# A four-layer graph network on one core: node work in two halves, two tables of range sums, clears at other places, empty tiles left out

## The chip, the cores and the metric

The kernel runs on one core of a Trainium2 chip. The metric is device time in microseconds (us) of one execution; a number of runs is given as the median of its executions. Engines are named as in the profile: PE (TensorE matmul), PEld (its weight loads), DVE (VectorE), ACT (ScalarE), POOL (GpSimd), SP (SyncE); "SPq" and "ACTq" are the instructions that start a transfer.

## What is computed

There are 12,500 nodes of 32 features and 400,000 edges, sorted by their destination dst. Each of four layers normalizes the nodes, forms a message for each edge from the source node's row, and adds the messages up by destination:

```python
h = relu(layernorm(x)); x = x + (1 + eps) * h + segment_sum(relu(h[src] + edge_attr_32), dst)      # layer 0
h = relu(layernorm(x)); x = x + L1(h, src, dst, edge_attr_3, edge_attr_10, edge_weight)            # layer 1
h = relu(layernorm(x)); x = x + L2(h, src, dst)                                                    # layer 2
h = relu(layernorm(x)); x = x + L3(h, src, dst, edge_attr_4, edge_attr_8)                          # layer 3
```

Layer 1 is an equivariant tensor product (tanh gates, weights of a small network on edge_attr_10, sums by dst). Layer 2 is a graph convolution with normalized degrees: `norm * (segment_sum((norm * h)[dst], src) + norm * h)`, `norm = rsqrt(1 + deg)`, where deg counts how often a node is a source; its sums go by source. Layer 3 is a product like layer 1's with a hidden layer of 256 and a factor 1 / sqrt(E / N).

## The kernel before

**Nodes.** x and h stay in SBUF as 125 partitions x 100 nodes x 32 features (`self.x`, `self.h`; `NP` = 125, `J` = 100). `norm_relu` (L415) is eight DVE operations and one ACT square over all of them, each of the large ones on 125 x 3200 elements; it ends with a store of h to a table `feats[l]` in HBM (L444), from which the edges gather rows. With `by_part` the features are stored in another order, by two copies (L440, L441).

**Edges.** They are cut into 196 windows of 16 tiles of 128 edges; four tiles are a group. There are 3125 tiles that hold edges; the last window has 5 of them. For each tile POOL issues one indirect transfer that gathers 128 rows (L617 in layer 0, L907 in the fused loop of layers 1 and 2, L1380 in layer 3); in layer 0, in most windows, the last two tiles are instead picked from a table in SBUF with 14 nodes to a line (`table`, L583 to L586, and `from_table`). In the fused loop POOL also issues one scatter with add per tile (L1108), to tables of layer 2 by source.

**Sums.** As the edges are sorted, a window's destinations lie in a range of at most 128 nodes. PE adds the messages of a window up with a one-hot matrix (`collect`, L468), and `put_late` (L495, transfer L498, on ACT's queue) writes 128 rows of the result to a table in HBM, `tabs[l][no % TABS[l]]`, at the window's first node. Neighbouring windows overlap, so they go to different tables: four in layers 0, 2 and 3, two in layer 1 (there `put`, L493, on SP). Tables are cleared first (`clear`, L393: five transfers of 125 x 640 zeros and a tail, L396 and L397, on ACT's queue). After a loop `gather_sum` (L448) loads the layer's tables, in turn on SP and ACT (L452), and adds them (L455); `end0`, `end1`, `end2` and `end3` add the sum to x (L1353 in layer 3), and `out` is stored at L1354.

**Order.** `setup` loads x; `norm_relu(0)` follows; `windows` (L256) loads dst (L265), works out each window's first node and a flag that says whether the fast form of the loops may run (widths and distances of windows, L284 to L304), and the program branches on it. In the branch `layer0` first takes four steps of the generator `rest`, the clears of layer 0's tables, and builds `table`; then it runs `edges` (L655). That loop loads two windows ahead, gathers four groups ahead, and takes one step of `rest` at each second group: the other ten tables' clears, then weights, places, unit vectors and parts of the embeddings for the later layers. The instructions of an engine are put in order by a scheduler that goes by their dependencies; for POOL in layer 3 the written order is kept. Then follow `norm_relu(1)`, `degrees`, the store of `mid` (x and degrees by node, L806), the fused loop `edges12`, `end1`, `norm_relu(2)` (which starts while layer 2's scatters still run), `end2`, `norm_relu(3)`, the loop `edges3`, `end3`. In `edges3` a window passes through `scalars`, `product` (L1425 to L1435), `outputs` (L1441 to L1449), `thirds` (L480 to L484), `collect` and `add`, in four steps each.

Of the kernel before, what the change touches and what calls it, by code (L numbers as in the profile page):

```python
# [16 lines left out]
P = 128  # L17
# [11 lines left out]
TABS = {0: 4, 1: 2, 2: 4, 3: 4}  # L29
ROUND = 12582912.0  # L30
PIECES = 5
# [30 lines left out]
class GNN:  # L62
# [47 lines left out]

    def rows_for(self, t, n, c, t0):

        k = max(0, min(n, self.filled(c) - t0))
        if k < n:
            self.nc.vector.memset(t[:, k:n, :], 0.0)
        return range(k)

    def nodes(self, ap):
        return ap.rearrange("(p j) d -> p (j d)", p=NP)


    def setup(self):
# [3 lines left out]
        nc.sync.dma_start(self.x.rearrange("p j d -> p (j d)"), self.nodes(self.a["x"]))  # L126
# [31 lines left out]

        self.none = keep.tile([P, D + 1], F32, name="none")
# [80 lines left out]
    def rest(self, pool):  # L240

        nc, J = self.nc, self.J
        zero = pool.tile([P, J * D // PIECES], F32, name="zero")
        nc.vector.memset(zero, 0.0)
        for l in range(4):
            for t in self.tabs[l][: TABS[l]] if self.fast else self.tabs[l]:
                self.clear(t, zero)
                yield
        yield from self.weights(pool)
        if self.fast:  # L250
            yield from self.places_by_edge(pool)
            yield from self.unit_vectors(pool)
            yield from self.parts_of(pool, self.a["ea10_c"], self.emb10)
            yield from self.parts_of(pool, self.a["ea8_c"], self.emb8)

    def windows(self):  # L256
# [4 lines left out]
        with ExitStack() as ctx:  # L261
# [3 lines left out]
            nc.scalar.dma_start(dst.rearrange("p w t -> p (w t)"), self.a["dst"])  # L265
            first = pool.tile([P, NW], F32, name="first")
# [29 lines left out]
            nc.vector.tensor_reduce(top[:, 0:1], loc, AX.XY, ALU.max)  # L296
# [9 lines left out]
            nc.vector.tensor_scalar(flag, worst, float(P), None, op0=ALU.is_lt)  # L306
        return nc.values_load(flag[0:1, 0:1], min_val=0, max_val=1)
# [85 lines left out]
    def clear(self, t, zero):  # L393
        n = self.J * D // PIECES
        for k in range(PIECES):
            self.nc.scalar.dma_start(self.nodes(t[: self.N])[:, n * k : n * k + n], zero[:NP])  # L396
        self.nc.scalar.dma_start(t[self.N :], zero[:, :D])  # L397

    def rsqrt(self, pool, v, shape):

        nc = self.nc
        n = v.shape[0]
        r = pool.tile(shape, F32, name="rs_r")
        t = pool.tile(shape, F32, name="rs_t")
        r, t = r[:n], t[:n]
        nc.scalar.activation(t, v, AF.Sqrt)
        nc.vector.reciprocal(r, t)
        nc.vector.tensor_mul(t, r, r)
        nc.vector.tensor_mul(t, t, v)
        nc.vector.tensor_scalar(t, t, -0.5, 1.5, op0=ALU.mult, op1=ALU.add)  # L410
        nc.vector.tensor_mul(r, r, t)
        return r


    def norm_relu(self, l, scale=None, by_part=False, store=True):  # L415


        nc, J = self.nc, self.J
        with self.tc.tile_pool(name=f"norm{l}", bufs=1) as pool:
            def wide(s):  # L420
                return s[:, :, None].to_broadcast([NP, J, D])

            m = pool.tile([NP, J], F32, name="m")
            nc.vector.tensor_reduce(m, self.x, AX.X, ALU.add)
            nc.vector.tensor_scalar_mul(m, m, 1.0 / D)
            nc.vector.tensor_tensor(self.h, self.x, wide(m), op=ALU.subtract)
            sq = pool.tile([NP, J, D], F32, name="sq")
            nc.scalar.activation(sq, self.h, AF.Square)
            v = pool.tile([NP, J], F32, name="v")
            nc.vector.tensor_reduce(v, sq, AX.X, ALU.add)  # L430
            nc.vector.tensor_scalar(v, v, 1.0 / D, 1e-5, op0=ALU.mult, op1=ALU.add)
            r = self.rsqrt(pool, v, [NP, J])
            if scale is not None:
                nc.vector.tensor_mul(r, r, scale)
            nc.vector.tensor_mul(self.h, self.h, wide(r))
            nc.vector.tensor_scalar_max(self.h, self.h, 0.0)
            h = self.h
            if by_part:
                h = sq
                nc.vector.tensor_copy(h[:, :, 0:8], self.h[:, :, 0:8])  # L440
                nc.vector.tensor_copy(h[:, :, 8:32].rearrange("p j (i u) -> p j u i", i=3),  # L441
                                      self.h[:, :, 8:32].rearrange("p j (u i) -> p j u i", i=3))
            if store:
                nc.sync.dma_start(self.nodes(self.feats[l][: self.N]), h.rearrange("p j d -> p (j d)"))  # L444

    def gather_sum(self, l, pool):

        nc = self.nc  # L448
        parts = []
        for k, t in enumerate(self.tabs[l][: TABS[l] if self.fast else NTAB]):  # L450
            s = pool.tile([NP, self.J, D], F32, name=f"part{k}")
            (nc.sync, nc.scalar)[k % 2].dma_start(s.rearrange("p j d -> p (j d)"), self.nodes(t[: self.N]))  # L452
            parts.append(s)
        for part in parts[1:]:
            nc.vector.tensor_add(parts[0], parts[0], part)  # L455
        return parts[0]


    def collect(self, l, pool, psum, c, feat, t0):
# [7 lines left out]
        for k in range(G):  # L467
            nc.tensor.matmul(c["sum"], lhsT=oh[:, k, :], rhs=feat[:, k, :], start=t0 + k == 0, stop=t0 + k == self.CT - 1)  # L468
        if t0 + G == self.CT:
# [4 lines left out]
    def thirds(self, pool, c, step):  # L474

        nc = self.nc
        if step == 0:
            c["f3"] = pool.tile([P, self.CT, 3, D], BF16, name="f3")
# [177 lines left out]
    def edges(self, load, gather, front, main, tail, begin=None, windowed=None, beside=None):  # L656
# [4 lines left out]
        with self.tc.For_i(0, self.T // IT, 1) as it:  # L661
            i = it * IT
            n = CPI * CG
# [3 lines left out]
            def fetch(g):  # L667
                c, k = divmod(g, CG)
                if k == 0:
                    for c1 in range(len(chunks), min(c + 1 + (LEAD if self.fast else 0), CPI)):  # L670
# [3 lines left out]
                        chunks[c1]["no"] = c1  # L674
                        if windowed:
# [32 lines left out]
    def layer0(self):  # L708
# [5 lines left out]
        with ExitStack() as ctx:  # L714
            rest = None
            if self.fast:
                self.resident(ctx)
                rest = self.rest(ctx.enter_context(tc.tile_pool(name="rest", bufs=1)))
                for _ in range(TABS[0]):
                    next(rest)  # L720
# [39 lines left out]
            def tail(c, t0, m):  # L760
# [21 lines left out]
                for k in range(G):  # L782
                    nc.tensor.matmul(c["deg"][:NP, :J], lhsT=ohi[:, k, :], rhs=olo[:, k, :],
                                     start=t0 + k == 0, stop=t0 + k == self.CT - 1)
                if t0 + G == self.CT:
# [6 lines left out]
        with tc.tile_pool(name="end0", bufs=1) as pool:  # L792
            agg = self.gather_sum(0, pool)
            nc.vector.tensor_add(self.x, self.x, agg)
            nc.vector.scalar_tensor_tensor(self.x, self.h, self.eps1, self.x, op0=ALU.mult, op1=ALU.add)

    def layers12(self):

        nc, J = self.nc, self.J
        self.norm_relu(1, by_part=True)  # L800
# [7 lines left out]
        self.end1()  # L808
        self.norm_relu(2, scale=self.deg, store=False)
        self.end2()  # L810

    def layer1(self):
        self.norm_relu(1)
        self.any1()
        self.end1()
# [9 lines left out]
    def end2(self):  # L825
        nc, J = self.nc, self.J
        with self.tc.tile_pool(name="end2", bufs=1) as pool:
            agg = self.gather_sum(2, pool)
            nc.vector.tensor_add(agg, agg, self.h)
            nc.vector.tensor_mul(agg, agg, self.deg[:, :, None].to_broadcast([NP, J, D]))  # L830
            nc.vector.tensor_add(self.x, self.x, agg)

    def end1(self):
        with self.tc.tile_pool(name="end1", bufs=1) as pool:
            self.nc.vector.tensor_add(self.x, self.x, self.gather_sum(1, pool))
# [476 lines left out]
    def layer2(self):  # L1312
        nc, tc = self.nc, self.tc
        self.degrees()
        self.norm_relu(2, scale=self.deg)
# [27 lines left out]
        self.end2()  # L1343

    def layer3(self):
        nc = self.nc
        with ExitStack() as ctx:
            if self.fast:
                self.resident(ctx)
            self.norm_relu(3, by_part=self.fast)  # L1350
            (self.edges3 if self.fast else self.any3)()
        with self.tc.tile_pool(name="end3", bufs=1) as pool:
            nc.vector.tensor_add(self.x, self.x, self.gather_sum(3, pool))  # L1353
        nc.sync.dma_start(self.nodes(self.out), self.x.rearrange("p j d -> p (j d)"))  # L1354

    def edges3(self):

        nc, tc, CT = self.nc, self.tc, self.CT
        with ExitStack() as ctx:
# [36 lines left out]
            def scalars(c, g, i):  # L1396

                if (g, i) == (0, 0):
                    c["q"] = wp.tile([P, CT, 16], F32, name="q", bufs=3)
                    c["dd"] = wp.tile([P, CT, 3, 8], F32, name="dd", bufs=3)  # L1400
                    c["vv"] = wp.tile([P, CT, 3, 8], F32, name="vv", bufs=3)
                gs = slice(G * g, G * g + G)
# [10 lines left out]
            def dots(c):  # L1413
                nc.vector.tensor_reduce(c["q"][:, :, 8:16], c["dd"].rearrange("p g k u -> p g u k"), AX.X, ALU.add)

            def product(c, g):

                if g == 0:
# [18 lines left out]
            def outputs(c):  # L1437
                sh = c["sh"]
                f = c["f"] = wp.tile([P, CT, D], F32, name="f")
                fv = f[:, :, 8:32]  # L1440
                nc.vector.tensor_reduce(f[:, :, 0:8], c["pa"], AX.X, ALU.add)  # L1441
                nc.vector.tensor_reduce(fv.rearrange("p g (w i) -> p g i w", i=3),  # L1442
                                        c["pv"].rearrange("p g i (w u) -> p (g i) w u", u=8), AX.X, ALU.add)
                rs = wp.tile([P, CT, 8], F32, name="rs", bufs=1)
                nc.vector.tensor_reduce(rs, c["ps"], AX.X, ALU.add)  # L1445
                t1 = wp.tile([P, CT, 8, 3], F32, name="t1", bufs=1)
                nc.vector.tensor_mul(t1, rs[:, :, :, None].to_broadcast([P, CT, 8, 3]),
                                     sh[:, :, None, 1:4].to_broadcast([P, CT, 8, 3]))
# [9 lines left out]
            def collect(c):  # L1458
                c["sum"] = ps.tile([P, B], F32, name="ps_sum")
                for k in range(CT):  # L1460
                    nc.tensor.matmul(c["sum"][: 3 * D, 0:P], lhsT=c["f3"][:, k].rearrange("p i f -> p (i f)"), rhs=c["oh"][:, k, :],  # L1461
                                     start=k == 0, stop=k == CT - 1)
# [22 lines left out]
            for c in range(NW + 1):  # L1485
# [3 lines left out]
                for s in range(4):  # L1489
# [5 lines left out]
                    if now:  # L1495
                        product(now, s)
                        places(now, 4 * s, 4 * s + 4)
# [173 lines left out]
```

## Time and profile before

| what | us |
|---|---|
| median of 4 runs | 18773.51 (18759.29 to 18782.71) |
| the profiled execution | 18764.26 |
| its span in the trace | 18762.5 |
| POOL busy in the span | 14661.1 (78%) |
| PE, DVE, ACT busy | 13498.4, 13656.4, 7248.7 |
| first gather of layer 0 / of the fused loop / of layer 3 | 74.33 / 3744.34 / 13924.30 |
| last put of layer 3, end of the span | 18680.32, 18762.5 |

The span is the time from the first to the last instruction of one profiled execution; the execution's own time is 1.8 us longer. Busy times of engines overlap. In lines of the timeline the columns are start (us), duration (us), engine, line of the kernel, operation, output<-inputs, count, and in brackets the idle time of the engine before it with what ended it ("issue": nothing that the profile shows). In lines of groups they are line, engine, operation, output<-inputs, count, then busy us and mean ns of one, then idle us before them with the main releaser.

### The profile page before, as it was taken

To read this page: it belongs to the slowest core of one execution; us is meant where nothing else is said; L and a number is where in the kernel's file an instruction comes from. 1 tells how busy PE (TensorE), PEld (TensorE's weight loads), DVE (VectorE), ACT (ScalarE), POOL (GpSimd) and SP (SyncE) were. 2 spreads that over 40 slices of the span, in tenths; PEclk is the share of its full clock that TensorE was granted. 3 is DMA by queue.
4 is the path that set the end of the run, shared out by engine and by line. 5 is a ranking of instruction groups with operands and counts; after the bars stand their busy time and mean duration, and the time that the engine had idled before them with its cause. 6 is when DMAs were issued, how large, how long until landed. Compare 5 with 4: busy or idle time off the path is not lost. (4 is left out here: it accounts for less than half of the span.)

```text
span 18762.5 us, 211174 instructions
## 1 busy us (share of the span) xinstructions
PE 13498.4 (72%) x64508; PEld 7139.8 (38%) x64508; DVE 13656.4 (73%) x26105; ACT 7248.7 (39%) x15398; POOL 14661.1 (78%) x14476
## 2 busy tenths in 40 slices
PE   5888888676666666666666666666638888888886
PEld 4555555422112121211111112111116666666665
DVE  6887766687777777777777777777747777777776
ACT  2334333233333333333333333333315555555554
POOL 5777777578888888888888888888868888888885
PEclk8888888787777777777777777777758888888888
DMA  4246422244444444444444444444431111111111
GB/s 123 64 121 194 141 38 38 48 106 92 94 92 94 91 91 92 92 94 92 94 91 91 92 91 93 93 95 91 88 63 27 26 27 26 27 26 27 26 27 33
DMA packets 1506892, 1429.22 MB, mean 76 GB/s; under 512 B 1053126, under 2 KB 1267796, under 8 KB 1452156
## 3 DMA queue, kind: packets, MB, share of 16 engines
q1 hardware_dynamic: 697752, 1170.64, 19.9%
q0 software_dynamic: 737712, 199.28, 13.6%
q10 hardware_dynamic: 70272, 45.63, 0.8%
q8 instruction: 512, 8.39, 0.2%
q14 instruction: 644, 5.28, 0.1%
HBM read 1177.50 MB, written 236.40 MB: 75 GB/s over the span
## 5 line engine op out<-in xcount | busy, mean ns | idle before, releaser
L1108 POOL DMA_INDIRECT acc<-summed,rows x3125 | 4995.5, 1599 | 993.7 <-issue 733.0
L1425 PE MATMUL ps_w<-w2b,hid 128*128 128x256 f32 x12544 | 3446.7, 433 | 833.5 <-DVE pv L1433 832.8
L907 POOL DMA_INDIRECT hs<-feat,src x3125 | 3135.6, 1003 | 1080.7 <-issue 930.6
L1380 POOL DMA_INDIRECT hs<-feat,src_all x3125 | 3053.5, 977 | 888.3 <-issue 784.4
L617 POOL DMA_INDIRECT hs<-feat,src_all x2741 | 2672.4, 975 | 940.7 <-issue 613.0
L948 PE MATMUL ps_y<-Q,w2t 64*128 64x512 f32 x4704 | 2097.6, 887 | 1806.5 <-DVE z L951 1796.9
L1425 PEld LDWEIGHTS ps_w<-w2b,hid 128*128 128x128 f32 x12544 | 2737.3, 221 | 1430.5 <-issue 872.9
L951 DVE TENSOR_TENSOR z<-ps_y,hid 128x1024 f32<-128x1024 f32 x2352 | 2852.7, 1213 | 328.1 <-PE ps_y L948 324.4
L605 PE MATMUL lined<-table,which 128*128 128x448 bf16 x8064 | 2041.1, 399 | 42.8 <-DVE picked L610 27.4
L958 PE MATMUL ps_o<-z,sums 128*32 128x512 f32 x9408 | 1955.5, 735 | 3.7 <-DVE r L963 3.2
L948 PEld LDWEIGHTS ps_y<-Q,w2t 64*128 64x128 f32 x4704 | 639.4, 261 | 2973.9 <-DVE z L951 2183.2
L922 DVE STREAM_TRANSPOSE X<-hs 128x512 f32<-128x512 f32 x392 | 270.0, 690 | 1986.8 <-DMA hs<-feat,src 1986.8
L480 ACT CAST f<-f 128x512 bf16<-128x512 f32 x784 | 479.9, 612 | 2908.1 <-DVE f L976 2671.0
L1393 ACT ACTIVATE hid<-ps_h 128x1024 f32<-128x1024 f32 x784 | 798.9, 1019 | 1670.7 <-PE ps_h L1391 1656.2
L932 ACT COPY X<-ps_m 32x512 f32<-32x512 f32 x784 | 451.5, 576 | 2553.3 <-PE ps_m L929 2522.4
L929 PE MATMUL ps_m<-has,win 128*32 128x512 f32 x1568 | 726.5, 1029 | 912.8 <-DVE has L916 772.1
L948 PE MATMUL ps_y<-X,w2t 64*128 64x512 f32 x4704 | 1260.0, 636 | 151.3 <-DVE z L951 150.2
L605 PEld LDWEIGHTS <-which 128*128 128x128 bf16 x8064 | 864.0, 117 | 703.6 <-issue 236.4
L1455 ACT ACTIVATE oh<-iota,local 128x128 bf16<-128x128 f32 x3136 | 1056.4, 391 | 49.0 <-DMA local<-local 25.9
L468 PEld LDWEIGHTS ps_win<-m,oh 128*128 128x128 f32 x6272 | 993.8, 234 | 182.3 <-issue 113.3
L983 ACT ACTIVATE oh<-iota,local 128x128 bf16<-128x128 f32 x3136 | 1014.9, 390 | 71.8 <-DMA local<-local 71.8
L468 PE MATMUL ps_win<-m,oh 128*128 128x32 f32 x6272 | 981.4, 306 | 61.9 <-DVE oh L465 33.7
(230 smaller groups left out, 21832.9 us busy)
## 6 DMA issues: line engine op xcount, KB each, us to landing
has<-loc_t SPq DMA_DIRECT2D x392, 1024.0 KB
srow<-in_src_t SPq DMA_DIRECT2D x392, 512.0 KB
N<-n_t SPq DMA_DIRECT2D x3136, 32.0 KB
hs<-feat,src_all POOLq DMA_INDIRECT x5866
emb<-pp SPq DMA_DIRECT2D x252, 280.0 KB
emb<-emb SPq DMA_DIRECT2D x196, 360.0 KB
emb<-pp SPq DMA_DIRECT2D x252, 224.0 KB
emb<-emb SPq DMA_DIRECT2D x196, 288.0 KB
```

What stands on the lines that cost most here:

```text
L468: nc.tensor.matmul(c["sum"], lhsT=oh[:, k, :], rhs=feat[:, k, :], start=t0 + k == 0, stop=t0 + k == self.CT - 1)
L605: nc.tensor.matmul(t, lhsT=c["which"][:, b, k * P : k * P + P], rhs=self.table3[:, b, i], start=(b, i) == (0, 0), stop=(b, i) == (BLOCKS - ...
L617: self.nc.gpsimd.indirect_dma_start(out=t[:, k, :], out_offset=None, in_=self.feats[l][:], in_offset=bass.IndirectOffsetOnAxis(ap=idx[:, t ...
L907: nc.gpsimd.indirect_dma_start(out=c["hs"][:, k, :], out_offset=None, in_=self.feats[1][:], in_offset=bass.IndirectOffsetOnAxis(ap=c["src" ...
L948: nc.tensor.matmul(y[:, q, :], lhsT=self.w2t[64 * q : 64 * q + 64, h, j, :], rhs=c["Q" if j < 3 else "X"][64 * q : 64 * q + 64, h, :], sta ...
L951: nc.vector.tensor_mul(z, y, c["hid"][:, 2 * h : 2 * h + 2, :])
L958: nc.tensor.matmul(c["o", j // 3][32 * q : 32 * q + 32, :], lhsT=self.sums[:, j, :], rhs=c["z", j, q % 2][:, q // 2, :], start=j % 3 == 0, ...
L983: nc.scalar.activation(c["oh"][:, k, :], self.iota, AF.Square, bias=c["local"][:, k : k + 1], scale=-1.0)
L1108: nc.gpsimd.indirect_dma_start(out=self.tabs[2][k % NTAB][:], out_offset=bass.IndirectOffsetOnAxis(ap=c["rows"][:, G * g + k : G * g + k + ...
L1380: nc.gpsimd.indirect_dma_start(out=c["hs"][:, k, :], out_offset=None, in_=self.feats[3][:], in_offset=bass.IndirectOffsetOnAxis(ap=c["src" ...
L1425: nc.tensor.matmul(w[:, k, :], lhsT=c["hid"][:, m, 4 * g + k].rearrange("p q s -> p (q s)"), rhs=self.w2b[:, m, :], start=m == 0, stop=m == 1)
L1455: nc.scalar.activation(c["oh"][:, k, :], self.iota, AF.Square, bias=c["local"][:, k : k + 1], scale=-1.0)
```

## The change

- `TABS` is {0: 2, 1: 2, 2: 4, 3: 2}: two tables in layers 0 and 3, 10 cleared in all in place of 14.
- x's load, the norm, the loads and sums of the tables, the stores of h and of the output go by two halves of 50 nodes to a partition (`halves`). `norm_relu` takes over the sum of the tables (`parts_in`, all loads on SP) and the addition to x; relu and scale are one operation, and with `by_part` four that also do the reordering.
- `windows` issues dst's load and then calls the first norm; one full reduce (L296) is replaced by one of a 128 x 196 array.
- Layer 0's two tables are cleared on ACT's queue before the flag is read; the other eight on SP's, as the last steps of `rest`, one transfer in two steps.
- `x += eps1 * h` of layer 0 stands before its loop in place of behind it; layer 2's own term is added by `own`, behind `norm_relu(2)`.
- In the last window of layers 0 and 3 groups without edges are left out (2 of 4).

The core of the diff:

```diff
-TABS = {0: 4, 1: 2, 2: 4, 3: 4}
+TABS = {0: 2, 1: 2, 2: 4, 3: 2}
+    def groups(self, c):
+
+        return max(1, -(-self.filled(c) // G))
+    def halves(self):
+        return slice(0, self.J // 2), slice(self.J // 2, self.J)
...
-        nc.sync.dma_start(self.x.rearrange("p j d -> p (j d)"), self.nodes(self.a["x"]))
+        for js in self.halves():
+            nc.sync.dma_start(self.x[:, js].rearrange("p j d -> p (j d)"), self.nodes(self.a["x"], js))
...
-        for l in range(4):
-            for t in self.tabs[l][: TABS[l]] if self.fast else self.tabs[l]:
-                self.clear(t, zero)
-                yield
         yield from self.weights(pool)
...
+        for l in range(4):
+            for t in self.tabs[l][2 if l == 0 else 0 : TABS[l] if self.fast else NTAB]:
+                for _ in self.clear(t, self.nc.sync):
+                    yield
+                    yield
...
             nc.scalar.dma_start(dst.rearrange("p w t -> p (w t)"), self.a["dst"])
+            meanwhile()
...
-            nc.vector.tensor_reduce(top[:, 0:1], loc, AX.XY, ALU.max)
+            nc.vector.tensor_reduce(top[:, 0:1], high, AX.X, ALU.max)
...
+        for t in self.tabs[0][:2]:
+            for _ in self.clear(t, nc.scalar):
+                pass
         return nc.values_load(flag[0:1, 0:1], min_val=0, max_val=1)
...
+    def norm_relu(self, l, add=None, scale=None, by_part=False, store=True):
...
+            parts = [self.parts_in(pool, add, u) if add is not None else () for u in range(2)]
+            for u, js in enumerate(self.halves()):
...
+                x, h = self.x[:, js], self.h[:, js]
+                for k, part in enumerate(parts[u][1:]):
+                    nc.vector.tensor_add(parts[u][0], parts[u][0], part)
+                if add == 2:
+                    nc.vector.tensor_mul(parts[u][0], parts[u][0], wide(self.deg[:, js]))
+                if add is not None:
+                    nc.vector.tensor_add(x, x, parts[u][0])
...
+                if by_part:
+                    turned = h[:, :, 8:32].rearrange("p j (u i) -> p j i u", i=3)
+                    for i in range(4):
+                        nc.vector.scalar_tensor_tensor(
+                            sq[:, :, 8 * i : 8 * i + 8], turned[:, :, i - 1] if i else h[:, :, 0:8], 0.0,
+                            r[:, :, None].to_broadcast([NP, n, 8]), op0=ALU.max, op1=ALU.mult)
+                    h = sq
+                else:
+                    nc.vector.scalar_tensor_tensor(h, h, 0.0, wide(r), op0=ALU.max, op1=ALU.mult)
+                if store:
+                    nc.sync.dma_start(self.nodes(self.feats[l][: self.N], js), h.rearrange("p j d -> p (j d)"))
...
+    def parts_in(self, pool, l, u):
...
+            self.nc.sync.dma_start(s.rearrange("p j d -> p (j d)"), self.nodes(t[: self.N], js))
...
-                for _ in range(TABS[0]):
-                    next(rest)
+            nc.vector.scalar_tensor_tensor(self.x, self.h, self.eps1, self.x, op0=ALU.mult, op1=ALU.add)
...
-        self.end1()
-        self.norm_relu(2, scale=self.deg, store=False)
-        self.end2()
+        self.norm_relu(2, add=1, scale=self.deg, store=False)
+        self.own()
...
-            agg = self.gather_sum(2, pool)
-            nc.vector.tensor_add(agg, agg, self.h)
-            nc.vector.tensor_mul(agg, agg, self.deg[:, :, None].to_broadcast([NP, J, D]))
-            nc.vector.tensor_add(self.x, self.x, agg)
+        nc.vector.tensor_mul(self.h, self.h, self.deg[:, :, None].to_broadcast([NP, self.J, D]))
+        nc.vector.tensor_add(self.x, self.x, self.h)
...
-            nc.vector.tensor_add(self.x, self.x, self.gather_sum(3, pool))
-        nc.sync.dma_start(self.nodes(self.out), self.x.rearrange("p j d -> p (j d)"))
+            parts = [self.parts_in(pool, 3, u) for u in range(2)]
+            for u, js in enumerate(self.halves()):
+                for part in parts[u]:
+                    nc.vector.tensor_add(self.x[:, js], self.x[:, js], part)
+                nc.sync.dma_start(self.nodes(self.out, js), self.x[:, js].rearrange("p j d -> p (j d)"))
...
             def product(c, g):
 
+                if g >= self.groups(c):
+                    return
...
-                for k in range(CT):
+                n = G * self.groups(c)
+                for k in range(n):
...
-        g.norm_relu(0)
-        ok = g.windows()
+        ok = g.windows(lambda: g.norm_relu(0))
```

## The prediction

> **What bounds the kernel now.** I read the costliest groups first. The four gather and scatter groups of POOL lead, and nearly all the idle time ahead of them is "issue", time in which POOL waited for nothing:
>
> ```profile
> POOL 5777777578888888888888888888868888888885
> L1108 POOL DMA_INDIRECT acc<-summed,rows x3125 | 4995.5, 1599 | 993.7 <-issue 733.0
> L907 POOL DMA_INDIRECT hs<-feat,src x3125 | 3135.6, 1003 | 1080.7 <-issue 930.6
> L1380 POOL DMA_INDIRECT hs<-feat,src_all x3125 | 3053.5, 977 | 888.3 <-issue 784.4
> L617 POOL DMA_INDIRECT hs<-feat,src_all x2741 | 2672.4, 975 | 940.7 <-issue 613.0
> ```
>
> The first line is POOL's busy tenths in 40 slices, the others give count, busy time, mean ns and idle time. In the timeline POOL's next instruction follows its last after 0.30 us. So inside the three edge loops POOL is full, and an edit there saves nothing unless it takes instructions from POOL. The change takes none of its 12,116 transfers away; in the order of the changed program POOL's sequence is the same, six small dropped calculations at the end apart. What can be won lies where POOL stands still: at the start, between the loops, after the last. The timeline shows these places, columns start, us, engine, line:
>
> ```profile
> 74.33 1.10 POOL L617 DMA_INDIRECT hs<-feat,src_all  x1 [72.49 <-DMA acc<-zero]
> ...
> 117.13 1.50 ACT L583 CAST table<-tv 128x448 bf16<-128x448 f32 x3 [85.58 <-DMA acc<-zero]
> ...
> 136.80 0.94 POOL L617 DMA_INDIRECT hs<-feat,src_all  x1 [32.51 <-DVE m L756]
> ...
> 3691.01 7.02 DVE L455 TENSOR_TENSOR part<-part,part 125x3200 f32<-125x3200 f32 x2 [16.80 <-DMA part<-acc]
> ...
> 3744.34 0.94 POOL L907 DMA_INDIRECT hs<-feat,src  x1 [129.45 <-ACT rs_t L406]
> ...
> 13766.97 5.34 POOL L1108 DMA_INDIRECT acc<-summed,rows  x1 [0.30 <-issue]
> ...
> 13867.64 7.02 DVE L455 TENSOR_TENSOR part<-part,part 125x3200 f32<-125x3200 f32 x2 [8.46 <-DMA part<-acc]
> ...
> 13924.30 1.01 POOL L1380 DMA_INDIRECT hs<-feat,src_all  x1 [103.89 <-DMA feat<-sq]
> ...
> 18735.80 7.02 DVE L455 TENSOR_TENSOR part<-part,part 125x3200 f32<-125x3200 f32 x2 [19.68 <-DMA part<-acc]
> ```
>
> POOL gathers from 74.33, stalls from 104.3 (its 24th gather issues at 103.35) to 136.8 because ACT's casts come late, stands from 3614.9 to 3744.3 and from 13820.4 to 13924.3, and the end follows the last sum (put at 18680.32) by 82 us. The time in these places is transfers of node arrays (125 partitions, 1.6 MB), so I looked at their rate in the table of stretches (last columns: DMA share, GB/s):
>
> ```profile
> 66.00:75.00 9.00, 0.00 (x0) 0.00 (x0) 1.55 (x12) 0.00 (x0) 0.67 (x1) 1.00 0.87 287
> 18683.00:18700.00 17.00, 0.00 (x0) 0.00 (x0) 0.00 (x0) 0.00 (x0) 0.00 (x0) 0.50 0.30 122
> ```
>
> The edge indices (128 partitions) moved at 287 GB/s; table loads with nothing beside them at 122 GB/s on 0.30 of the DMA engines, though SP and ACT both issued. A single store (out, 18746.4 to 18762.5, and feat, 3729.98 to 3743.6) needed 13.6 to 16 us. So a table costs 13.1 us, half a table 6.6, on one queue or two. The Trainium skill ("DMA: Bandwidth & Descriptors", section "Bandwidth") gives 341 GB/s at 1 MB; by that the two tables dropped at the end would be worth 9 us, not 26. Its measurement is with 128 partitions, the row with 125 decides.
>
> **Part A, the start.** Now ACT sends 24 clears of four tables from 66.33, and its casts for the table of lines wait until 117.13; the gathers hang on these from the 25th on. As 24 are done by then, POOL's effective start is 136.80 − 24 × 1.25 = 106.8. In the changed program dst is loaded ahead of the first norm, only two tables are cleared, ahead of the flag, and no clear stands ahead of the casts. x's second half lands at about 16.9 as x does now; with the first half's work done meanwhile, the norm's DVE work (16.88 to 38.91 now, less 1.83 for the fused relu) ends near 33. The flag's chain (45.42 to 64.65, 19.2 us, less 3.1: a reduce of 3.41 becomes one of 196 columns) then ends near 49. Flag to first gather takes 9.7 now: 59; plus 4 for clears that share the engines with the feat store: 63. Casts need 19.7 us from ACT free to gather (117.13 to 136.80), so they end near 75, ahead of the 24th gather (63 + 30 = 93): no stall. Gain 106.8 − 63 = 44, less 5 for table arithmetic on DVE beside gathers: **−39** (−48 without these 5 and the 4; −27 if POOL stalls 12 us more for the casts).
>
> **Part B, first loop to second.** Now: last gather done at 3614.9, last sum put at 3631.59, first part load issued 2.0 later, 6.4 MB in until 3691.0, 39 us of DVE work, store 13.6, gather at 3744.3: 129.4 us after the last gather. Changed, counted from the last gather: put at 11 (six us earlier, as two empty groups are not worked through), loads at 15, two tables as four half loads, first halves in at 30, second at 43. The merged order has half 0's sum and mean first, then waits for half 1's add, so little of half 0 runs ahead. From 43: about twelve half operations of 1.75 (half of 3.49, estimate), twice 2.2 of small ones, the copies for the order of parts now within the multiply; the two chains interleave. Half 0 stored from 55, half 1 from 63, landed 70, gather at 72.5. The product h·eps1 (3.49) goes ahead of the first loop, where DVE idles. **−57** (−45 if half 1's chain is not interleaved with half 0's square on ACT, −68 if half 0 runs ahead). POOL's one wait in the ramp behind it, 21.8 us for L1104, is due to a has load that SP issues at 3763.7, behind the mid store; in the new order it stands ahead of the feat store: **−5** (0 to −10).
>
> **Part C, second to third.** All four tables stay, now in eight half loads on SP, behind table 0's wait (issued 13831.46 now; ACT started its two 10 us earlier). Behind that wait on SP stand only the feat store and the third loop's loads, which come later anyway. In at 13831.5 + 6.4 MB / 122 GB/s = 13884, 17 us later than now; behind it half 1's share alone: nine half operations and small ones, 18, store 6.8 + 2: gather at 13911 against 13924.3, −13. Against it, own() puts two full DVE operations with two SBUF inputs in POOL's drain. Beside such operations a scatter took 5.34 (and 4.64, 4.56, 3.86) in place of 1.54: 2 × 3.4 = +7. **−6** (−16 to +8, if table 0's halves wait longer or half 1 is not helped).
>
> **Part D, the end.** Last put about 10 earlier: two of four product groups gone, and the last window's reductions (2.27 + 3.34 + 1.21 + 0.56 + 0.56 us) halved. Then loads 2.7 after the put as now, 3.2 MB in 26.4 and landing: 18701; two half adds 3.5, half a store 6.8 with half 0's in front of it done by then: about 18710 against 18762.5. **−52** (−40 to −60, as table 0 may start before the last put).
>
> **Costed at nothing.** Eight late clears, 40 transfers of 0.32 MB on SP: in the new order they stand between the edge loads of windows 9 to 14, not at the end of the loop. They take 12.8 MB / 121 GB/s = 106 us; SP runs five windows ahead (5 × 17.5 = 87), so at worst POOL stalls 19 us once. Two tables in place of four mean that a put waits for the one two windows before: 35 us, with a landing of 2.65 (put 18680.32, load 18682.97). Groups left out elsewhere lie under POOL.
>
> **Sum** −39 − 57 − 5 − 6 − 52 = **−159** (ends −104 and −202). The profiled run took 18764.3 (span 18762.5), 9 below the median of the four, 18773.5; so 18605 for a run like the profiled one, and **18614** for the median.
>
> The skill speaks against the halves ("DMA: Bandwidth & Descriptors", section "Rules for kernel authors"): transfers to halves serialise on the same engines, so don't split. The trace agrees on the engines (0.30 and 122 GB/s for two queues), but splits by partitions are meant; here the second half's transfer hides the first half's arithmetic. If splitting brought nothing, the sum would be about −115.
>
> **Rivals.**
> (1) The change does only part of what it says: halves interleave on DVE so that none runs ahead, and the "late" clears, hoisted, stall the first loop. Halves are worth 5 (A), 15 (B), 15 (C), 10 (D) by the working above; with the stall of 19: −159 + 45 + 19 = −95, **18679**. For it: half 0 waits for half 1's add in the order of part B, and SP waits for lanes in the first loop even now. Against: the last store is half as long in any order.
> (2) Slower: POOL's rows lengthen. The same gather costs 975, 977 and 1003 ns in three loops, so what stands beside it counts. Place: all 12,116 transfers; 28 ns each, the spread of these rows, is +339, so +180 net, **18954**. It decides from 159 / 12,116 = 13 ns, and is slower beyond the bound from 16. Against it: POOL's order and DVE's work inside the loops are unchanged.
> (3) The start's gain is given back, because the first loop is held by preparation on DVE or SP (77 gathers in 100 us from 1200 to 2200, 80 from 2300 to 3500, where 0.95 + 0.30 us apiece fills POOL): −120, **18654**, inside the range.
>
> **Chances.** The forecast (−125 to −200) 0.70; smaller gain, (1) and (3), 0.21; still larger 0.02; nothing left 0.03; rival (2) 0.04. Under about 0.2% (37 us) this kernel can't be told from no change: faster 0.93, same 0.03, slower 0.04. Range 18570 to 18690: the sum's ends, −202 and −104, and from there to rival (1).
>
> **What would show it.** Right: first gather near 63 and no second start; two part loads per half after 3570; about 72 us without POOL between the first loops, some 97 between the next two (after scatters stretched twice more); the last put to the end 40 us. Wrong: a POOL gap between windows 9 and 20 behind clears (1); the means of L617, L907, L1108, L1380 up by 10 ns (2); POOL's gather count per 100 us lower in the first loop (3).

## The result, and the profile after

The changed kernel takes 18797.64 us (median of 40 runs) against 18776.29 (60 runs) for the kernel before: a ratio of 1.001, 95% interval 1.0006 to 1.0015. The forecast was 18614, so 184 us are missing. By the prediction's own limit of 37 us the result counts as no change, to which it gave 0.03. The profiled execution of the changed kernel spans 18781.7 us, 19.2 more than before. POOL's groups on its page, to be laid beside the four of the prediction:

```profile
L1120 POOL DMA_INDIRECT acc<-summed,rows x3125 | 5113.0, 1636 | 957.5 <-issue 729.6
...
L919 POOL DMA_INDIRECT hs<-feat,src x3125 | 3147.9, 1007 | 1080.4 <-issue 945.2
L1395 POOL DMA_INDIRECT hs<-feat,src_all x3125 | 3055.0, 978 | 867.6 <-issue 867.6
L641 POOL DMA_INDIRECT hs<-feat,src_all x2741 | 2669.9, 974 | 939.7 <-issue 615.5
```

Counts are the same, and three of the means are within 4 ns of before. The scatters of the fused loop (L1120, L1108 before) went from 1599 to 1636 ns. That is 117 us on the engine that bounds that loop. The timeline at the places of the prediction:

```profile
79.56 1.23 POOL L641 DMA_INDIRECT hs<-feat,src_all  x1 [77.72 <-DVE tv L608]
...
265.58 0.94 POOL L641 DMA_INDIRECT hs<-feat,src_all  x1 [16.31 <-DVE lo L801]
...
3689.60 0.94 POOL L919 DMA_INDIRECT hs<-feat,src  x1 [78.18 <-DMA local<-local]
...
13993.61 1.01 POOL L1395 DMA_INDIRECT hs<-feat,src_all  x1 [83.42 <-issue]
...
18741.78 0.34 ACTq L522 DMA_DIRECT2D acc<-wsum  x1
...
18768.62 1.82 DVE L1368 TENSOR_TENSOR x<-x,part 125x1600 f32<-125x1600 f32 x1 [4.14 <-DMA part<-acc]
```

The second start (POOL stood 32.5 us ahead of 136.80 in the kernel before) is gone, but POOL now stands 16.3 us ahead of 265.58. Both idle stretches of POOL between the loops are shorter, and the end follows the last put by 40 us, not 82. Cut where POOL's first and last transfers of each loop begin, the two spans compare so:

| stretch (us) | before | changed | difference | forecast |
|---|---|---|---|---|
| start to last gather of the first loop | 3613.95 | 3610.48 | -3.5 | -39 |
| to first gather of the fused loop | 130.4 | 79.1 | -51.3 | -57 |
| fused loop, to its last scatter | 10074.5 | 10219.0 | **+144.5** | -5 (ramp) and +7 (own()) |
| to first gather of the third loop | 105.4 | 85.0 | -20.5 | -13 |
| third loop, to POOL's last operation | 4694.4 | 4694.3 | -0.1 | 0 |
| to the last put, to the end | 61.7 + 82.2 | 53.9 + 39.9 | -50.0 | -52 |

So the forecast gains between the loops and at the end are there. A loop that was forecast to stay as it is took 144.5 us of them back, and the first loop most of the start's.

### The profile page after: what moved, and what is told of

It reads as the page before. It is cut to its first block, busy times and chain, and to the rows that moved or that the text cites. A ratio compares the mean times of both kernels' runs of the same rounds, so it can differ in the third digit from the quotient of the medians.

```text
span 18781.7 us, 211231 instructions
## 1 busy us (share of the span) xinstructions
PE 13410.0 (71%) x64444; PEld 7062.2 (38%) x64444; DVE 13607.1 (72%) x26138; ACT 7225.1 (38%) x15394; POOL 14788.7 (79%) x14470
## 5 line engine op out<-in xcount | busy, mean ns | idle before, releaser
L1120 POOL DMA_INDIRECT acc<-summed,rows x3125 | 5113.0, 1636 | 957.5 <-issue 729.6
L1111 PE MATMUL ps<-hd,eq 128*128 128x96 bf16 x3128 | 315.4, 234 | 2307.8 <-DVE eq L1097 2274.1
L970 PE MATMUL ps_o<-z,sums 128*32 128x512 f32 x9408 | 1819.1, 680 | 87.0 <-DVE rows L1106 81.7
L1111 PEld LDWEIGHTS <-eq 128*128 128x128 bf16 x3128 | 184.7, 109 | 3033.8 <-DVE eq L1097 2459.1
L960 PEld LDWEIGHTS ps_y<-Q,w2t 64*128 64x128 f32 x4704 | 561.9, 227 | 1513.7 <-DVE z L963 748.6
L1476 ACT ACTIVATE oh<-iota,local 128x128 bf16<-128x128 f32 x3128 | 1053.8, 391 | 36.5 <-DMA edge_attr<-in_edge_attr 13.8
```

The source lines that it names most:

```text
L960: nc.tensor.matmul(y[:, q, :], lhsT=self.w2t[64 * q : 64 * q + 64, h, j, :], rhs=c["Q" if j < 3 else "X"][64 * q : 64 * q + 64, h, :], sta ...
L970: nc.tensor.matmul(c["o", j // 3][32 * q : 32 * q + 32, :], lhsT=self.sums[:, j, :], rhs=c["z", j, q % 2][:, q // 2, :], start=j % 3 == 0, ...
L1120: nc.gpsimd.indirect_dma_start(out=self.tabs[2][k % NTAB][:], out_offset=bass.IndirectOffsetOnAxis(ap=c["rows"][:, G * g + k : G * g + k + ...
L1476: nc.scalar.activation(c["oh"][:, k, :], self.iota, AF.Square, bias=c["local"][:, k : k + 1], scale=-1.0)
```

## The cause, looked for in the trace

In the fused loop of the changed kernel 100 scatters take more than 2.4 us, before 4. One of them in the timeline (DVE and POOL, other engines left out):

```profile
5015.96 1.21 DVE L963 TENSOR_TENSOR z<-ps_y,hid 128x1024 f32<-128x1024 f32 x1
...
5017.10 0.15 DVE L1106 TENSOR_TENSOR rows<-far,src 128x4 int32<-128x4 f32 x1
5017.17 0.68 DVE L508 TENSOR_TENSOR f<-f,f 128x512 bf16<-128x512 f32 x1
5017.31 2.58 POOL L1120 DMA_INDIRECT acc<-summed,rows  x1 [0.30 <-DVE rows L1106]
5017.77 0.68 DVE L947 TENSOR_TENSOR Q<-N,X 128x512 f32<-128x512 f32 x1
5018.37 0.55 DVE L1116 TENSOR_REDUCE summed<-ps 128x128 f32<-128x384 f32 x1
```

The scatter begins 0.14 us into L508, the last step of splitting the messages into three bf16 parts, an operation with both inputs in SBUF; L947, the product Q and another such operation, follows with no gap. The scatter ends at 5019.89, that is 1.44 after L947's end at 5018.45. In the kernel before the same Q operation has a reduce behind it, and the scatter ends 1.46 after the Q operation alone:

```profile
5044.11 0.69 DVE L935 TENSOR_TENSOR Q<-N,X 128x512 f32<-128x512 f32 x1
5044.20 2.06 POOL L1108 DMA_INDIRECT acc<-summed,rows  x1 [0.30 <-issue]
5044.73 0.68 DVE L1090 TENSOR_REDUCE cnt<-tmp 128x4 f32<-128x512 bf16 x1
```

From 5000 to 5800 of the changed kernel's span, all 27 scatters above 1.7 us end 1.44 to 1.50 after the end of such an operation, while operations that read one input from PSUM (z, eq, tmp, has) stretch none. The Trainium skill ("SBUF — State Buffer", section "Who interferes with whom") states that a DVE instruction with two SBUF inputs contends with a GpSimd instruction that reads SBUF. The rows agree.

The pair L508 and L947 holds a scatter through both operations, in 125 of 125 cases of the loop (scatters that begin at least 0.1 us ahead of L508's end). That is no general rule. Here the scatter begins under L1091, L985 follows with no gap, both have two SBUF inputs, and the scatter ends 1.44 after L1091 alone, as it does in all 93 cases of this pair:

```profile
5010.30 0.68 DVE L1091 TENSOR_TENSOR hd<-hd,hd 128x512 bf16<-128x512 f32 x1
5010.56 1.86 POOL L1120 DMA_INDIRECT acc<-summed,rows  x1 [0.30 <-issue]
5010.89 0.55 DVE L985 TENSOR_TENSOR f<-f,r 128x384 f32<-128x384 f32 x1
```

Why the one pair holds to its end and the other does not stays open. For the sum it is L508 that counts: 133 scatters of the loop begin under it, and they alone take 117 us more than 1.58 apiece; before, 32 begin under the same operation (L484), for 8 us more.

DVE does the same 73 operations per window in both kernels, but in another order: in the changed one L508 and a Q stand together behind the row numbers that release a scatter. The theory: the order in which the scheduler interleaves DVE in the fused loop costs the 144 us, and what changed the order is the pool (the block of SBUF from which tiles are taken) in which layer 0's tables are loaded and summed. Before, this was a pool closed ahead of the norm; now it is the norm's own. The rival: the loop is slower for what is done around it (halves, two tables, clears on SP).

## The experiments

Each was timed against the kernel before on its own chip: e1 to e4 on one, e5 to e8 on a second, e9 to e11 on a third, e12 on a fourth. On the first two the first loop took 4226 to 4292 us in place of some 3540 (the granted clock between 500 and 3500 us is 0.78 in e1 and e7, 0.83 in the profile before), so between chips only ratios and stretches are compared.

**e1, the sum in a pool of its own**

```diff
-        self.norm_relu(1, add=0, by_part=True)
+        with self.tc.tile_pool(name="end0", bufs=1) as pool:
+            parts = [self.parts_in(pool, 0, u) for u in range(2)]
+            for u, js in enumerate(self.halves()):
+                for part in parts[u]:
+                    self.nc.vector.tensor_add(self.x[:, js], self.x[:, js], part)
+        self.norm_relu(1, by_part=True)
```

> The changed kernel, with one thing moved: the half loads of layer 0's two tables and their sums stand in a pool of their own that is closed ahead of the norm, as before, and not in the norm's pool. Same operations, same halves. Theory (the pool decides in which order the scheduler interleaves DVE in the fused loop; in the changed order one scatter a window starts under two back-to-back DVE operations with two SBUF inputs and waits for both): DVE's order in the fused loop is that of before again, the scatters' mean falls from 1636 to about 1600 ns, the loop from 10219 to about 10075 us, and the time from 18797 to about 18655. Rival (the fused loop is longer for what is done around it: tables in halves, clears on SP, the phase of the start): scatters stay at 1636 ns and the time at 18797.

Measured: ratio 0.9912 (0.9897 to 0.9927). Six scatters above 2.4 us; fused loop 10173.9 us. That is a somewhat larger gain than the 0.9936 that 18655 would be.

**e2, the kernel before with its sum in the norm's pool**

```diff
+            if add is not None:
+                nc.vector.tensor_add(self.x, self.x, self.gather_sum(add, pool))
+                nc.vector.scalar_tensor_tensor(self.x, self.h, self.eps1, self.x, op0=ALU.mult, op1=ALU.add)
             m = pool.tile([NP, J], F32, name="m")
...
-        self.norm_relu(1, by_part=True)
+        self.norm_relu(1, by_part=True, add=0)
```

> The kernel before, with one thing moved: layer 0's four tables are loaded and summed in the norm's pool. Nothing else of the change. Theory: DVE's order in the fused loop becomes that of the changed kernel, the scatters' mean goes from 1599 to about 1636 ns, and the time from 18776 to about 18915. Rival (the order is not the cause): 18776, scatters at 1599.

Measured: ratio 1.0061 (1.0047 to 1.0074), 115 us slower than the kernel before on that chip; some 139 were expected. The scatter groups of e1 and of e2, one line each:

```profile
L1125 POOL DMA_INDIRECT acc<-summed,rows x3125 | 5015.8, 1605 | 1021.7 <-issue 762.0
```

```profile
L1107 POOL DMA_INDIRECT acc<-summed,rows x3125 | 5112.9, 1636 | 971.0 <-issue 757.4
```

The one edit gives the old kernel the new kernel's scatters, and its undoing gives the new kernel the old one's. On that chip e2's fused loop is 137.8 us longer than e1's (10311.7 against 10173.9). The rival falls: halves, tables and clears of e1 are those of the changed kernel. The order itself can be read in the traces. Between 6000 and 12000 us every window of a kernel has the same sequence of 73 DVE operations, and only two sequences occur: that of the changed kernel, which e2, e5 and e6 have too, and that of the kernel before, which e1 and all the others have. Why the place of a pool changes what the scheduler does behind it was not studied.

**e5, the same order with one operand moved.** The pool and order are the changed kernel's. The kernel leaves out the last step of the split: in place of the second bf16 part it subtracts a constant in PSUM.

```diff
-            nc.vector.tensor_tensor(c["f3"][:, :, 2, :], c["f"], c["f3"][:, :, 1, :], op=ALU.subtract)
+            nc.vector.tensor_tensor(c["f3"][:, :, 2, :], c["f"], c.get("flat", c["f3"][:, :, 1, :]), op=ALU.subtract)
...
+                c["flat"] = before[:, None, 0:D].to_broadcast([P, CT, D])
```

> The changed kernel, with its pool as it is; in the fused loop the last of the three splits of the messages (L508) takes its second operand from a constant in PSUM in place of SBUF, so that part of the split is left out. DVE's order is that of the changed kernel, and the operation has the same size. Theory (a scatter that begins under an operation with two SBUF inputs waits for its end, and for the next one's that follows without a gap): the scatters of 2.58 us, one in about half the windows, begin under L508 no longer and fall to 1.6 to 1.9; the scatters' mean falls by 25 to 40 ns, the fused loop by 80 to 140 us, and so the time. Rival (the order as such costs, through PE or the sequence of waits): scatters stay at about 1636 ns, time as the changed kernel's.

**e6 and e7, the changed kernel and the kernel before as they are, beside e5**

> The changed kernel as it is, to be beside the others on one chip. All theories: within 0.2% of the kernel before.

> The kernel before as it is, for its profile on the same chip. All theories: its fused loop is shorter than the changed kernel's by about 140 us, all other stages are longer or equal.

Measured: e5 19472.22 us, e6 19585.14, the kernel before 19618.51 (ratios 0.9929, 0.9915 to 0.9943; and 0.9984, 0.9975 to 0.9993). The scatters of e5 and e6:

```profile
L1121 POOL DMA_INDIRECT acc<-summed,rows x3125 | 4985.8, 1595 | 957.0 <-issue 770.2
```

```profile
L1120 POOL DMA_INDIRECT acc<-summed,rows x3125 | 5119.3, 1638 | 957.3 <-issue 747.8
```

With order and sizes as they were, and one operand read from PSUM, scatters above 2.4 us fall from 109 to 6, all six in the last 60 us of the loop, and the fused loop falls from 10298.0 to 10188.1 us: 110 of the 113 us between the two medians. In e6 129 scatters begin under L508 and take 2.50 us on average, in e5 118 begin under it and none takes more than 1.60. L508 itself takes 0.68 us in both. It no longer needs ACT's copy of the part before, but in neither kernel is there a gap ahead of it. So it is the operand, not the sequence of waits. e7's fused loop (one run) is 10194.1, 104 below e6's where about 140 were expected; on this chip the changed kernel's other gains are just larger than that loss.

**e3 and e4, the clears.** e3 is e1 with the late clears really late: their zeros are made from degree sums, so that they go out from 3174 to 3929 us and not from 196 to 322 as in e1.

```diff
+                if self.fast:
+                    self.nc.vector.tensor_scalar_mul(held[:NP, :600].rearrange("p (j d) -> p j d", d=6),
+                                                     self.deg[:, :, None].to_broadcast([NP, J, 6]), 0.0)
+                    self.nc.vector.tensor_scalar_mul(held[:NP, 600:], self.deg[:, :40], 0.0)
-                for _ in self.clear(t, self.nc.sync):
+                for _ in self.clear(t, self.nc.sync, held if self.fast else None):
```

> e1, and the eight late clears copy zeros that DVE makes out of the degree sums (times 0), so that the scheduler can't put them ahead of windows 9 to 14. Theory (the clears on SP's queue delay ACT's weight copies and with them the first loop's work, the stalls of 16.3 and 6.0 us at 249 and 302): the stalls go, last gather of the first loop about 26 us earlier, time about 26 below e1, near 18628. Rival (ACT's own copies of weights stall it): as e1.

e4 is e3 with layer 0's clears behind the third edge load, on SP, in place of ahead of the flag:

```diff
-        for t in self.tabs[0][:2]:
-            for _ in self.clear(t, nc.scalar):
-                pass
...
+                    if self.loads == LEAD + 1:
+                        for t in self.tabs[0][:2]:
+                            for _ in self.clear(t, nc.sync):
+                                pass
```

> e3, and the two clears of layer 0's tables stand on SP's queue behind the third edge load, not on ACT's ahead of the flag. Theory (these clears hold src_all's load, which was issued at 58.1 and landed 20 us later): first gather from 79.6 to about 62, time about 17 below e3, near 18611. Rival (the feat store and the loads of the table of lines end last anyway): first gather stays above 75, time as e3.

Measured: e3 0.9913 (0.9900 to 0.9927), no different from e1, so its expectation failed there; a stall of 19.0 us at 300 in e1 is absent in e3, but on that chip POOL waits some 3 us in every window of the first loop anyway, and the loop is only 11 us shorter. e4 0.9894 (0.9879 to 0.9910), first gather at 60.2, as expected; its median is 30 below e3's, where 17 were expected.

**e8 and e12, e4 again on other chips; e9, e1 again**

> The kernel of e4 once more (own pool, late clears held, no clears in front), beside the changed kernel. Theory: 1.0 to 1.2% below the kernel before; of it 140 us from the order in the fused loop and some 20 from the start. Rival (e4's gain belonged to that chip): below 0.5%.

> The kernel of e1 once more, as the ground for e10 and e11 on one chip. All theories: about 0.9% below the kernel before.

> The kernel of e4 and e8 a third time, for a chip on which the first loop is bound by POOL, as in the profiles of before and of the change (first loop about 3540 us; 4230 to 4290 on the two other chips). Theory: there the stalls of 18.0 and 4.0 us at 264 and 305 are gone and the first gather comes near 60, so that the first loop's last gather is some 35 us earlier than in e9 and the ratio to before about 0.990. Rival (the late clears cost nothing, and the start is given back later in the loop): ratio 0.992 as e9.

Measured: e8 0.9895 (0.9879 to 0.9910). e9 18618.71 us, 0.9921 (0.9907 to 0.9934). e12 18582.22 us, 0.9896 (0.9880 to 0.9913). On chips with the short first loop the expected difference of e12 and e9, some 35 us, is there: the gain over the kernel before on the same chip is 193 us in e12 and 149 in e9, though the intervals of the two ratios overlap a little. e9 stalls 18.0 and 4.0 us at 264 and 305 and starts at 76.6; e12 shows no stall above 3 us and this start:

```profile
59.94 1.16 POOL L645 DMA_INDIRECT hs<-feat,src_all  x1 [58.10 <-DMA src_all<-in_src]
```

Its first loop's last gather comes at 3569.3, 44 us ahead of e9's. What stalled there is in the waits of ACT between 200 and 310 in the changed kernel (waited for, us in total, times, longest):

```profile
ACT which L618 <- DMA acc<-zero: 22.1, 3, 11.0
ACT wsum L495 <- DMA w1tk<-wp: 19.1, 1, 19.1
ACT m L782 <- DMA acc<-zero: 12.9, 1, 12.9
...
ACT which L620 <- DMA local<-local: 9.4, 1, 9.4
```

The clears are issued by SP, but ACT has to send copies of weights (L404) between its own operations, these wait behind the clears, and the relu of the messages (m L782) and the one-hots of the table (which) stand behind them on ACT. The last row is a load that SP issued at 290.14, among the clears; it stands ahead of the second, shorter stall. That the clears cause the stalls is shown by e3 and e12; the way over ACT is read from these waits and has no experiment of its own.

**e10, no halves; e11, four tables at the end**, both on the kernel of e9. Of e10 the main line is shown; the loops over `u` go to one part to match.

```diff
-        return slice(0, self.J // 2), slice(self.J // 2, self.J)
+        return (slice(0, self.J),)
```

```diff
-TABS = {0: 2, 1: 2, 2: 4, 3: 2}
+TABS = {0: 2, 1: 2, 2: 4, 3: 4}
```

> e9 without halves: node work, table loads and stores over all 100 nodes of a partition at once, still two tables, still all on SP. By the prediction's terms halves are worth 5 at the start, 15 and 15 between the loops and 10 at the end, 45 in all: time 45 above e9. Rival (transfers are halved in size but not in sum, and halves interleave on DVE): within 15 of e9.

> e9 with four tables of sums in layer 3 in place of two, in halves. Theory: the last put to the end grows by two tables at 122 GB/s, 26 us, less what is loaded before the last put: 20 to 26, time 20 to 26 above e9, nothing else moves. Rival (end bound by sums and stores): below 10.

Measured: e10 18646.30 us, 0.9935 (0.9922 to 0.9949), 28 above e9, between the expected 45 and its rival's 15; e11 18663.61, 0.9944 (0.9930 to 0.9958), 45 above e9, more than the 20 to 26 expected. By the profiled spans the differences are 12 and 29, e9's profiled run being its slowest. By the stretches, halves are worth 14 us between the second and third loop, 4 between the first two, and some 6 at the end, where the prediction had 15, 15 and 10; at the start they cost, where it had a gain of 5: the first gather comes at 69.6 without them and at 76.6 with them. e11's end follows its last put by 68.5 us against 38.6 in e9. That is 30, a little above the 20 to 26 expected: the last sum begins 54.5 us after the last put (25.2 in e9), and half 0's store, issued at 18625.3, goes out while loads of half 1 are still under way. The rest of the 45 between the medians is in no stretch of the traces and stays open.

## Why the prediction was wrong

**The step that failed** is the one that cost the inside of the fused loop at nothing: "an edit there saves nothing unless it takes instructions from POOL", and, against rival (2), "POOL's order and DVE's work inside the loops are unchanged". POOL's order was unchanged, and so was the set of DVE's operations. Their sequence was not, and had not been compared. Rival (2) named the place (POOL's rows lengthen), and it is what happened, at one of the four rows: 37 ns on 3125 scatters is 117 us, 12 more on the gathers of that loop and a net 15 of waits make the 144.5. Spread over all 12,116 transfers the rows grew by 10.6 ns, just under the 13 at which rival (2) was to decide. It had been given a chance of 0.04. The trace held the warning: the scatters of 4.64, 3.86, 4.56 and 5.34 us, used only to price own(), began under DVE operations with two SBUF inputs, and the first three of them end 1.42 to 1.43 after these (L455, L835, L426). Read as a rule, those rows would have made DVE's sequence a term of the sum.

**Part A**, −39: measured −3.5 at the loop's last gather. The flag came at 50.3 as worked out (49), and no second start. But src_all, issued at 58.1 behind the clears, landed 20.5 us later, not 8.8, so the first gather stood at 79.6, not 63; e12 shows 59.9 without these clears. Then the late clears, costed at nothing with a bound of 19, stall POOL for 16.3 and 6.0 us. Rival (1) had named such a stall and priced it at 19, by loads that SP issues too late; by the waits it came mainly over ACT, which the prediction did not cost, and a late load of SP had a part in the second. Rival (3) did not come: from the first gather to the last, stalls left out, the first loop takes 3508 us before and 3510 changed.

**Part B**, −57: −51, of which e10 gives 4 to the halves and not 15. The further −5 did not come. The first has load of the fused loop (L899) is issued at 3706.47, still behind the feat and mid stores; those ahead of the feat store are the other ones (L1070), and they stood there before too (L1058). The ramp's one wait of 21.8 us became six, 53.0 in all within the loop's first 270 us. That is 31 more, with 15 less at the loop's end; in e9, with the old order, the ramp is back at one wait of 27.2. On the chip of e6 and e7 the ramps wait alike (121 and 128 us), so the loops differ less there, by 104.

**Part C**, −6: the gap shrank by 20.5, more than the 13 of its first term. own()'s two operations stretched two scatters to 3.22 us, 3.4 in all and not 7, because these began in the middle of the operations; the norm's halves stretched two more to 3.14, in place of the four long ones of before.

**Part D**, −52: −50.

**Sum.** Without the fused loop the changed kernel gained 3.5 + 51.3 + 20.5 + 0.1 + 50.0 = 125.4 us by the table, of 161 forecast there (39 + 57 + 13 + 52); the shortfall is part A's 35.5, the other differences cancel. With the loop's order given back (e9), the time is 18618.71 on a chip where the kernel before takes 18767.85: a gain of 149, near the forecast's 159. That nearness is in part luck: e9's first loop ends where it ended before (last gather at 3613.64 against 3613.95), so part A is still missing in it, and its profiled run, its slowest, spans only 130 us less than the profile before.

Two readings in the prediction were off, without bearing on its sum: from 1200 to 2200 us POOL issues 75 gathers in 100 us, not 77, and in the stretch at 287 GB/s loads of the table of lines and clears were issued beside the edge indices.

## What to carry to other kernels

When one engine is full and its instructions are held by another's, the sequence of the other engine is part of the cost: compare it window by window, not only by counts, whenever an edit touches anything ahead of an unrolled loop, be it only the pool in which a tile lives. A transfer is to be costed also with the engines that wait to issue theirs behind it, not only with the queue that it is on. And a change that gains nothing may be two changes of opposite sign; cut both spans at the same instructions before looking for a single cause.

## What was not expected of the hardware

A scatter that begins under a DVE operation with two SBUF inputs ends some 1.45 us after it (27 of 27 above 1.7 us between 5000 and 5800; its own time is 1.54 to 1.58). If a second such operation follows without a gap it can wait for that as well: 2.58 us under L508 and L947, of 0.68 each, in 125 of 125 cases, but not under L1091 and L985, in 93 of 93. A constant in PSUM as the second operand of L508 takes the delay under it away (no more than 1.60 us in 118 cases). Two of the chips ran the same first loop some 20% slower, at a granted clock of 0.78 against 0.83; why it is so much was not studied.
